# More gathers replaced by single-row copies on the SP and ScalarE queues, row addresses shifted ahead on VectorE, a 127-row load cut in two, and a small operand moved to PSUM

## The chip, the core and the metric

The kernel runs on one core of a Trainium2 chip. A core has five engines with an instruction queue each: TensorE (PE in the profile, with its weight loads as PEld), VectorE (DVE), ScalarE (ACT), GpSimd (POOL) and SyncE (SP)[...]. SP, ACT and POOL can issue DMAs. The metric is device time in microseconds (us) of one execution; lower is better. "Before" is the kernel without the change, "after" the one with it.

## What is computed

A layer norm, a two-layer graph network and a residual, on 12,500 nodes of 128 features and 200,000 edges sorted by destination. From the reference, cut:

```python
h = jnp.maximum(_layernorm(x), 0.0)                       # the network's node_features
wsum = segment_sum(edge_weight_raw, dst); deg = segment_sum(ones, dst)
w = edge_weight_raw / jnp.maximum(wsum, EPS)[dst]
feat = relu(node_features @ W_pool + b_pool)
msg = feat[src] * w[:, None]
neigh = where(deg > 0, segment_max(msg, dst), 0.0)
rst = node_features @ W1_self + neigh @ W1_neigh + b1
h = relu(rst / jnp.maximum(norm(rst), EPS))
neigh2 = segment_sum(h[src] * w[:, None], dst) / jnp.maximum(deg, 1.0)
out = x + relu(h @ W2_self + neigh2 @ W2_neigh + b2)
```

All is in float32. Twice, a row of 512 bytes is fetched for each of the 200,000 edges: `feat[src]` in layer 1, `h[src]` in layer 2.

## The kernel before

The program has three stages, each with an order of instructions written out by hand (`manual_schedule`). An engine executes its own instructions in that order; engines wait for each other by semaphores that the framework sets from the tiles' use.

**Preparation.** Nodes are taken in 25 groups of up to 4 x 128. Turn `i` of the loop at line 380 starts group `i` and finishes group `i - 3`. DVE takes mean and variance (L417, L418), writes the negative mean to `offs` (L422), and a turn later multiplies it by the reciprocal deviation (L400, L402); ACT takes the deviation (L420) and applies both (`xn`, L406); PE transposes and multiplies by W_pool; DVE adds the bias (`fb`, L385); POOL takes the maximum with 0 (`fr`, L388, three buffers); SP stores it to the table `feat_d` in HBM (L389). Beside this, DVE prepares edge lists (`edges1`, from L216 on). The lists lie 512 edges to a partition. `load_edges` (L119) loads them; the first 128 rows of `dst` are one row (L116) and a piece of 127, because each row carries its neighbours' values. They stand on ACT's queue between the loads of `src` and of the weights, while SP loads x (L132).

**Layer 1.** Edges are taken in 391 groups of 512, a group as 4 chunks of 128. In turn `i`, POOL issues the indirect gathers of group `i` (L503), each of which fetches 128 rows of `feat_d` by the indices in `srcT`; the tiles `gt` have 8 buffers. ACT multiplies by the edge weight (`gs`, L629), PE transposes, and DVE runs a scan with maximum (L636) that takes a mask from `kt`, which SP loads for each group, 4 turns ahead (L601). In later turns the last element of each segment is moved to its node's column: DVE makes a selection matrix (`sel`, L653), PE multiplies, ACT copies into `agg` (L678). Each fourth turn or so, when 128 nodes are whole, `nodes1` begins the node's part as a chain of six pieces, one a turn; in the fourth of them SP stores `h` to the table `h_d` (L551). Background jobs on the edge lists run on DVE in odd turns.

**Layer 2** has the same gathers from `h_d`, DVE makes `s` from the weights and positions (L711, L713), PE multiplies (`pa`, L731), DVE adds into `agg` (L736), and `nodes2` stores the result (L573). A last part, for inputs out of the expected form, is skipped at run time.

**Rows.** `Rows` (L456) spares POOL some gathers. For certain groups the first chunk is fetched by 128 single-row DMAs into a tile `ga` (two buffers). `load` of the 128 source indices into `ri` is L495; a queue then reads 8 of them into registers (L487), and for each computes the row's place and issues a copy of one row (L491). `every`, the distance of such groups, is 24 in layer 1 (SP alone) and 10 in layer 2 (SP and ACT, half each). The copies of a group are spread over the `every - 2` turns that begin `every` turns ahead. Their call stands at the head of a turn. Eight semaphores serve all DMAs of SP and ACT in rotation: a copy waits until the one eight places before it in the program has landed.

Of the kernel before, what the change touches and what calls it, by code (L numbers as in the profile page):

```python
# [7 lines left out]
F32 = mybir.dt.float32  # L8
BF16 = mybir.dt.bfloat16
I16 = mybir.dt.int16  # L10
I32 = mybir.dt.int32
AF = mybir.ActivationFunctionType
OP = mybir.AluOpType
# [4 lines left out]
P = 128  # L18
D = 128
G = 512  # L20
Q = 4
# [6 lines left out]
SLOW_B = 64  # L28
RB = 8
BL = 8  # L30
# [4 lines left out]
def gnn_kernel(ctx, tc, x, src, dst, ew, w_pool, b_pool, w1s, w1n, b1, w2s, w2n, b2, out):  # L35
# [13 lines left out]
    nc = tc.nc  # L49
    N = x.shape[0]  # L50
    E = src.shape[0]
    HI = -(-N // P)
# [3 lines left out]
    NG = GF + 1  # L56
# [56 lines left out]
    def load_edges(eng, a, tl, lead, t):  # L113
        o, k, row = t * P * G, min(P, GF - t * P), 0
        if lead and t == 0:
            eng.dma_start(tl[0:1, 0, 1:], a[None, 0:G + 1])  # L116
            row, o, k = 1, G, k - 1
        if k > 0:
            eng.dma_start(  # L119
                tl[row:row + k, t, :],  # L120
                bass.AP(tensor=a.tensor, offset=a.offset + o - lead, ap=[[G, k], [1, G + 2 * lead]]))
        if t == NT - 1:
            r = GF % P
            eng.dma_start(tl[r:r + 1, t, :TAIL + lead], a[None, E - TAIL - lead:E])
# [48 lines left out]
    shift = {}  # L173
# [206 lines left out]
    for i in range(len(groups) + 3):  # L380
# [16 lines left out]
        if at[1]:  # L397
            t0, n = at[1]
            rstd = rstds.pop(i - 1)
            nc.vector.reciprocal(rstd, rstd)  # L400
            off = offs.pop(i - 1)
            nc.vector.tensor_tensor(off, off, rstd, OP.mult)  # L402
            xn = wk.tile([P, Q, D], F32, name="xn")
# [6 lines left out]
        if at[0]:  # L410
# [9 lines left out]
            nc.scalar.activation(rstd, mv[:, :, 1], AF.Sqrt, bias=eps)  # L420
            offs[i] = wk.tile([P, Q], F32, name="off")
            nc.vector.tensor_scalar(offs[i], mv[:, :, 0], -1.0, None, op0=OP.mult)  # L422
# [33 lines left out]
    class Rows:  # L456


        def __init__(self, pool, table_d, every, engines):
            self.pool, self.table_d, self.every, self.engines = pool, table_d, every, engines  # L460
            self.tiles, self.todo, self.index = {}, [], {}

        def takes(self, g):
            return g >= 2 * self.every and g % self.every == 0 and g < NG - 16

        def tile(self, g):
            return self.tiles.pop(g)

        def turn(self, i):

            span = self.every
            g = i + span
            if self.takes(g):
                ga = self.tiles[g] = self.pool.tile([P, D], F32, name="ga", bufs=2)
                ri = self.index.pop(g)
                each = P // len(self.engines)
                self.todo = []
                for r in range(0, each, RB):
                    for e, eng in enumerate(self.engines):
                        self.todo.append((eng, ri, ga, e * each + r))  # L480
                self.steps = [len(self.todo) * k // (span - 2) for k in range(span - 1)]
            now = []
            if self.todo:
                n = self.steps[1] - self.steps[0]
                now, self.todo, self.steps = self.todo[:n], self.todo[n:], self.steps[1:]
            for eng, ri, ga, r in now:
                _, at = nc.values_load_multi_w_load_instructions(  # L487
                    ri[0:1, r:r + RB], [eng.engine], min_val=0, max_val=N - 1,
                    skip_runtime_bounds_check_because="sources of edges are nodes, as the gathers have it")
                for k in range(RB):  # L490
                    eng.dma_start(ga[r + k:r + k + 1, :], self.table_d[bass.ds(at[k], 1), :])  # L491
            g = i + span + 1
            if self.takes(g):
                self.index[g] = self.pool.tile([1, P], I32, name="ri", bufs=1)
                nc.sync.dma_start(self.index[g], src[None, g * G:g * G + P])  # L495

# [35 lines left out]

    def nodes1(wk, ps, t, nT, store):

# [14 lines left out]
        nc.vector.tensor_scalar(h, r, 0.0, ss, op0=OP.max, op1=OP.mult)  # L549
        if store:  # L550
            nc.sync.dma_start(h_d[t * P:(t + 1) * P, :], h)  # L551
        yield
        ph = ps.tile([P, P], F32, name="pn")
        nc.tensor.transpose(ph, h, ident)
# [25 lines left out]
    with tc.manual_schedule(), tc.tile_pool(name="ew", bufs=3) as wk, \  # L580
# [31 lines left out]
        carry = NEG  # L612
        byrow = Rows(wk, feat_d, 24, [nc.sync])
        for i in range(max(turn) + 6):
            byrow.turn(i)
            node_stage(5)
            if i + AHEAD < NG:
# [45 lines left out]
            if i in turn:  # L663
                n = turn[i]
                st = nodes1(wk, ps, n, agg[:, n * P:(n + 1) * P], True)
                next(st)
                busy[i + 1, 1] = st
# [12 lines left out]
            if 0 <= g < NG:  # L680
# [3 lines left out]
                for j, k in chunks:  # L684
                    nc.tensor.matmul(pas[g], rows[:k, j, :], sel[:k, j, :], start=j == 0,  # L685
                                     stop=j == len(chunks) - 1)
            node_stage(2)
            if i % 2:
                side_step()
        assert not busy  # L690
        i = NG
# [3 lines left out]
    with tc.manual_schedule(), tc.tile_pool(name="ew2", bufs=3) as wk, \  # L695
# [6 lines left out]
        late = None  # L702
        byrow = Rows(wk, h_d, 10, [nc.sync, nc.scalar])
        for i in range(max(turn) + 2):
            byrow.turn(i)
            if i < NG:
                gts[i] = gather(gp, h_d, i, byrow)
# [150 lines left out]
```

## Time and profile before

| | |
|---|---|
| runs | 4005.57, 4009.53, 4017.18 us; median 4009.53 |
| profiled execution | 4009.92 us, span 4007.7 us (2.2 us around it) |
| first gather of layer 1, first of layer 2, end of the last | 108.7, 2088.7, 3995.6 us |
| busy: PE, PEld, DVE, ACT, POOL | 59%, 44%, 42%, 22%, 74% |
| PE's clock, mean granted | 0.512 |
| HBM traffic | 73 GB/s over the span |
| gathers | 1549 of `feat_d`, 1527 of `h_d` |
| row copies | SP 1792 of `feat_d` and 2304 of `h_d`; ACT 2304 of `h_d` |

A group of the profile is a source line, an engine, an operation, the tiles it writes and reads, and how often it ran; behind the bar stand the busy time, the mean in ns, and the engine's idle time before it with what ended that. "issue" means that the engine waited for nothing the profile shows. SPq and ACTq are the queues' sequencers, which wait, compute registers and issue DMAs; this is not in the engines' busy time. In the view of one line the durations are least, median and greatest in ns, followed by the first and last start in us.

### The profile page before, as it was taken

What the parts mean: (1) busy time and instruction counts of PE and PEld (TensorE: products, weight loads), DVE (VectorE), ACT (ScalarE), POOL (GpSimd) and SP (SyncE); (2) the same over time, 40 slices, a digit from 0 to 9 for tenths busy, and PEclk for the clock granted to TensorE, in tenths of its full rate; (3) what the DMA queues carried; (4) which work ended last, traced back from release to release, by engine and by line L of the source; (5) the groups of instructions that cost most, each with busy time, mean ns of one, the idle gap of its engine ahead of it and who ended that gap; (6) DMA issues with size and microseconds to landing.
All of it is one profiled execution on the core that took longest, in us unless ns stands there. A gap on an engine that the chain in (4) does not pass through costs nothing. (4 is left out here: it accounts for less than half of the span.)

```text
span 4007.7 us, 52674 instructions
## 1 busy us (share of the span) xinstructions
PE 2370.1 (59%) x8349; PEld 1781.3 (44%) x8349; DVE 1670.9 (42%) x4620; ACT 889.9 (22%) x2907; POOL 2982.5 (74%) x3135
## 2 busy tenths in 40 slices
PE   6566666666666666666655555555555555555555
PEld 4344444444444444444444444444444444444444
DVE  8566666666666655555551111122121212112111
ACT  6344443444444444444430000000000000000000
POOL 4777777777777777777767777777777777777776
PEclk8555555555555555555555555555555555555555
DMA  5333333333333333333322222222222222222222
GB/s 150 88 81 84 81 82 82 81 81 83 82 84 82 82 83 84 83 84 83 83 62 59 61 61 62 61 62 62 61 62 61 62 61 61 62 62 61 61 61 55
DMA packets 238964, 295.25 MB, mean 74 GB/s; under 512 B 67603, under 2 KB 188228, under 8 KB 238614
## 3 DMA queue, kind: packets, MB, share of 16 engines
q0 software_dynamic: 98432, 201.72, 19.0%
q1 hardware_dynamic: 134868, 87.97, 8.0%
q10 hardware_dynamic: 5314, 2.11, 0.2%
q14 instruction: 278, 2.28, 0.2%
q8 instruction: 72, 1.18, 0.1%
HBM read 271.75 MB, written 19.77 MB: 73 GB/s over the span
## 5 line engine op out<-in xcount | busy, mean ns | idle before, releaser
L503 POOL DMA_INDIRECT gt<-feat_d,srcT x1549 | 1490.2, 962 | 474.2 <-issue 413.3
L503 POOL DMA_INDIRECT gt<-h_d,srcT x1527 | 1441.7, 944 | 483.1 <-issue 435.9
L731 PE MATMUL pa<-s,gt 128*128 128x48 f32 x3054 | 979.6, 423 | 840.7 <-DMA gt<-h_d,srcT 764.4
L731 PEld LDWEIGHTS pa<-s,gt 128*128 128x128 f32 x3054 | 765.1, 312 | 1057.8 <-DMA gt<-h_d,srcT 844.0
L630 PE MATMUL pm<-ident,gs 128*128 128x128 f32 x1563 | 681.2, 463 | 748.8 <-ACT gs L629 738.4
L629 ACT ACTIVATE gs<-gt,ewT 128x128 f32<-128x128 f32 x1549 | 608.3, 400 | 1007.7 <-DMA gt<-feat_d,srcT 995.2
L636 DVE TENSOR_TENSOR_SCAN pm<-kt,carry,pm 128x512 f32<-128x512 bf16 x390 | 502.0, 1287 | 728.5 <-PE pm L630 726.7
L630 PEld LDWEIGHTS pm<-ident,gs 128*128 128x128 f32 x1563 | 316.4, 208 | 1065.6 <-ACT gs L629 1054.9
L736 DVE TENSOR_TENSOR agg<-pa,agg 128x48 f32 x391 | 81.4, 208 | 1505.9 <-PE pa L731 1031.8
L685 PEld LDWEIGHTS pa<-sel,rows 128*128 128x128 f32 x1564 | 374.5, 329 | 34.5 <-ACT agg L678 34.1
L685 PE MATMUL pa<-sel,rows 128*128 128x48 f32 x1564 | 377.0, 390 | 0.9 <-ACT agg L678 0.9
L673 PE MATMUL pr<-ident,sc 128*128 128x128 f32 x782 | 246.8, 419 | 0.0
L653 DVE TENSOR_SCALAR sel<-cols,lastT,invT 128x48 f32<-128x48 f32 x782 | 206.7, 316 | 0.0
L645 DVE COPY_PREDICATED sc<-kt,pm 128x256 f32<-128x256 int16 x391 | 173.1, 443 | 13.3
L673 PEld LDWEIGHTS pr<-ident,sc 128*128 128x128 f32 x782 | 170.7, 227 | 0.1
L644 DVE COPY sc<-pm 128x256 f32<-128x256 f32 x391 | 162.1, 415 | 0.0
L713 DVE TENSOR_TENSOR s<-hit,w2T 128x192 f32<-128x192 f32 x391 | 139.7, 357 | 13.5
L660 ACT ACTIVATE rows<-pr 128x256 f32<-128x256 f32 x392 | 142.6, 364 | 1.0 <-PE pr L673 1.0
L711 DVE TENSOR_TENSOR hit<-iota,locT 128x192 f32<-128x192 f32 x391 | 139.1, 356 | 0.1
L678 ACT ACTIVATE agg<-pa 128x48 f32 x391 | 79.8, 204 | 140.1 <-PE pn L531 136.7
L530 PE MATMUL pn<-w_2s,hT 128*128 128x128 f32 x196 | 74.4, 484 | 0.0
L640 DVE COPY carry<-pm 128x1 f32<-128x1 f32 x390 | 61.6, 158 | 13.4
(143 smaller groups left out, 1274.2 us busy)
## 6 DMA issues: line engine op xcount, KB each, us to landing
kt<-keep_d SPq DMA_DIRECT2D x390, 128.0 KB
ga<-h_d SPq DMA_DIRECT2D x2304, 0.5 KB
ga<-h_d ACTq DMA_DIRECT2D x2304, 0.5 KB
ga<-feat_d SPq DMA_DIRECT2D x1792, 0.5 KB
gt<-feat_d,srcT POOLq DMA_INDIRECT x1549
gt<-h_d,srcT POOLq DMA_INDIRECT x1527
h_d<-h SPq DMA_DIRECT2D x98, 64.0 KB
xr<-in_x SPq DMA_DIRECT2D x97, 64.0 KB
```

The lines of the kernel that those rows point to most:

```text
L503: nc.gpsimd.indirect_dma_start(out=gt[:k, j, :], out_offset=None, in_=table_d[:, :], in_offset=bass.IndirectOffsetOnAxis(ap=srcT[:k, t, j, ...
L629: nc.scalar.activation(gs[:k, j, :], rows_j, AF.Copy, scale=ewT[:k, t, j, r:r + 1])
L630: nc.tensor.transpose(pms[i][:, j * P:j * P + k], gs[:k, j, :], ident[:k, :k])
L636: nc.vector.tensor_tensor_scan(pm[:, :ne], kt[:, :ne], pm[:, :ne], carry, op0=OP.add, op1=OP.max)
L644: nc.vector.tensor_copy(sc[:, :ne // 2], two[:, :, 1])
L645: nc.vector.copy_predicated(sc[:, :ne // 2], new[:, :, 1], two[:, :, 0])
L653: nc.vector.tensor_scalar(sels[g][:k, j, :], cols[:k, 1, :], lastT[:k, t, j, r:r + 1], invT[:k, t, j, r:r + 1], op0=OP.is_equal, op1=OP.mult)
L660: nc.scalar.activation(rws[g][:k, j, :], pr[:k, j, :], AF.Copy)
L673: nc.tensor.transpose(prs[g][:k, j, :], sc[:, j * P:j * P + k], ident)
L685: nc.tensor.matmul(pas[g], rows[:k, j, :], sel[:k, j, :], start=j == 0, stop=j == len(chunks) - 1)
L713: nc.vector.tensor_tensor(ss[i], hit, w2T[:, t, :, r:r + 1].to_broadcast([P, Q, LW]), OP.mult)
L731: nc.tensor.matmul(pas[g], rows_j, s[:k, j, :], start=j == 0, stop=j == len(chunks) - 1)
```

## The change

1. `Rows` takes each twelfth group in layer 1 from group 12 on (96 rows by SP in batches of 8, 32 by ACT in batches of 4), and each eighth in layer 2 from group 8 on (64 and 64, in batches of 8). Groups are taken up to 386. The batches are spread over all `every` turns that begin `every + 1` turns ahead. In layer 1 ACT's batches stand at the end of a turn; in layer 2 both queues' stand at its head.
2. The row numbers are shifted left by 9 on DVE, two turns before the first is used there, so that a queue reads the byte's place and issues the copy with it, both sides viewed as bytes. Two halves of one tile hold the lists in turn.
3. `load_edges` issues a list as a part of a multiple of 16 rows and a rest: the 127 rows become 112 and 15.
4. In the preparation the negative mean is written to PSUM, and the product with the reciprocal deviation to a new tile in SBUF.
5. The store of `h` comes one piece later, but for the last four node groups.

```diff
-        if k > 0:
-            eng.dma_start(
-                tl[row:row + k, t, :],
-                bass.AP(tensor=a.tensor, offset=a.offset + o - lead, ap=[[G, k], [1, G + 2 * lead]]))
+        for n in (k // 16 * 16, k % 16):
+            if n > 0:
+                eng.dma_start(
+                    tl[row:row + n, t, :],
+                    bass.AP(tensor=a.tensor, offset=a.offset + o - lead, ap=[[G, n], [1, G + 2 * lead]]))
+            o, row = o + n * G, row + n
...
-            off = offs.pop(i - 1)
-            nc.vector.tensor_tensor(off, off, rstd, OP.mult)
+            off = wk.tile([P, Q], F32, name="off")
+            nc.vector.tensor_tensor(off, offs.pop(i - 1), rstd, OP.mult)
...
-            offs[i] = wk.tile([P, Q], F32, name="off")
+            offs[i] = ps.tile([P, Q], F32, name="neg")
...
+        def __init__(self, pool, table_d, every, share):
+            self.pool, self.every, self.share = pool, every, share
+            self.bytes = table_d[:, :].bitcast(U8).rearrange("n b -> (n b)")
+            self.tiles, self.index, self.plan = {}, {}, {}
+            self.ri = pool.tile([64, P], I32, name="ri", bufs=1)
+            for g in range(every, NG - 4, every):
+                first = g - every - 1
+                at = 0
+                for eng, n, rb in share:
+                    for s in range(n // rb):
+                        turn = max(first + s * every // (n // rb), 0)
+                        self.plan.setdefault(turn, []).append((g, eng, at, rb))
+                        at += rb
+            self.turn(-2)
+            self.turn(-1)
...
         def takes(self, g):
-            return g >= 2 * self.every and g % self.every == 0 and g < NG - 16
+            return g % self.every == 0 and self.every <= g < NG - 4
+
+        def turn(self, i):
+            for g, lead, step in ((i + self.every + 2, -1, self.shift), (i + self.every + 3, -2, self.load)):
+                if i == lead:
+                    step(self.every)
+                elif i >= 0 and g > self.every and self.takes(g):
+                    step(g)
+
+        def load(self, g):
+            r = g // self.every % 2 * 32
+            self.index[g] = self.ri[r:r + 1, :]
+            nc.sync.dma_start(self.index[g], src[None, g * G:g * G + P])
+
+        def shift(self, g):
+            nc.vector.tensor_scalar(self.index[g], self.index[g], ROW_SHIFT, None, op0=OP.logical_shift_left)
+
+        def rows(self, i, engine):
+            for g, eng, r, rb in self.plan.get(i, ()):
+                if eng is not engine:
+                    continue
+                if g not in self.tiles:
+                    self.tiles[g] = self.pool.tile([P, D], F32, name="ga", bufs=2)
+                ga, ri = self.tiles[g].bitcast(U8), self.index[g]
+                _, at = nc.values_load_multi_w_load_instructions(
+                    ri[0:1, r:r + rb], [eng.engine], min_val=0, max_val=(N - 1) << ROW_SHIFT, ...)
+                for k in range(rb):
+                    eng.dma_start(ga[r + k:r + k + 1, :], self.bytes[None, bass.ds(at[k], 4 * D)])
...
-        if store:
+        if store and t >= HI - 4:
             nc.sync.dma_start(h_d[t * P:(t + 1) * P, :], h)
         yield
+        if store and t < HI - 4:
+            nc.sync.dma_start(h_d[t * P:(t + 1) * P, :], h)
...
-        byrow = Rows(wk, feat_d, 24, [nc.sync])
+        byrow = Rows(wk, feat_d, 12, [(nc.sync, 96, 8), (nc.scalar, 32, 4)])
         for i in range(max(turn) + 6):
             byrow.turn(i)
+            byrow.rows(i, nc.sync)
...
             node_stage(2)
+            byrow.rows(i, nc.scalar)
             if i % 2:
                 side_step()
...
-        byrow = Rows(wk, h_d, 10, [nc.sync, nc.scalar])
+        byrow = Rows(wk, h_d, 8, [(nc.sync, 64, 8), (nc.scalar, 64, 8)])
         for i in range(max(turn) + 2):
             byrow.turn(i)
+            byrow.rows(i, nc.sync)
+            byrow.rows(i, nc.scalar)
```

More of the change, by code (lines that the diff above doesn't have):

```diff
@@ L11 @@
 I32 = mybir.dt.int32
+U8 = mybir.dt.uint8
 AF = mybir.ActivationFunctionType
@@ L28 @@
 SLOW_B = 64
-RB = 8
+ROW_SHIFT = 9
 BL = 8
@@ L456, in gnn_kernel @@
     class Rows:
-        def __init__(self, pool, table_d, every, engines):
-            self.pool, self.table_d, self.every, self.engines = pool, table_d, every, engines
-            self.tiles, self.todo, self.index = {}, [], {}
-        def takes(self, g):
-            return g >= 2 * self.every and g % self.every == 0 and g < NG - 16
+        def __init__(self, pool, table_d, every, share):
[3 more added lines that the diff above has]
+            self.ri = pool.tile([64, P], I32, name="ri", bufs=1)
+            assert sum(n for _, n, _ in share) == P
+            for g in range(every, NG - 4, every):
[8 more added lines that the diff above has]
+            self.turn(-1)
@@ new lines, in shift @@
+        def shift(self, g):
[8 more added lines that the diff above has]
+                _, at = nc.values_load_multi_w_load_instructions(
+                    ri[0:1, r:r + rb], [eng.engine], min_val=0, max_val=(N - 1) << ROW_SHIFT,
+                    skip_runtime_bounds_check_because="sources of edges are nodes, as the gathers have it")
+                for k in range(rb):
+                    eng.dma_start(ga[r + k:r + k + 1, :], self.bytes[None, bass.ds(at[k], 4 * D)])
@@ L466, in tile @@
         def tile(self, g):
             return self.tiles.pop(g)
[L469 to L495, printed above, removed]
@@ L531, in linear, with nodes1 @@
         return nc.tensor.matmul(po, nT, W[neigh_w], start=False, stop=True)
-    def nodes1(wk, ps, t, nT, store):
+    def nodes1(wk, ps, t, nT, store=True):
         po = ps.tile([P, D], F32, name="pn")
@@ L664, in gnn_kernel @@
                 n = turn[i]
-                st = nodes1(wk, ps, n, agg[:, n * P:(n + 1) * P], True)
+                st = nodes1(wk, ps, n, agg[:, n * P:(n + 1) * P])
                 next(st)
```

## Prediction

> **What bounds the kernel now.** I read the page's groups first, for the engine that is busiest and for what its idle time waits on.
>
> ```profile
> L503 POOL DMA_INDIRECT gt<-feat_d,srcT x1549 | 1490.2, 962 | 474.2 <-issue 413.3
> L503 POOL DMA_INDIRECT gt<-h_d,srcT x1527 | 1441.7, 944 | 483.1 <-issue 435.9
> ```
>
> GpSimd (POOL) issues 3076 indirect gathers of 128 rows. Busy and idle time of the two groups add up to 1964 and 1925 us, nearly the whole span, and the idle part is "issue": it waits for nothing. The timeline of layer 2 shows the beat.
>
> ```profile
> 3035.51 0.94 POOL L503 DMA_INDIRECT gt<-h_d,srcT  x1 [0.30 <-issue]
> 3036.76 0.95 POOL L503 DMA_INDIRECT gt<-h_d,srcT  x1 [0.30 <-issue]
> 3038.01 0.94 POOL L503 DMA_INDIRECT gt<-h_d,srcT  x1 [0.31 <-issue]
> ```
>
> A gather each 1.249 us, 0.94 busy and 0.30 between. From start to start over all gathers the trace gives a mean of 1.249 in layer 2 (longest 1.27) and 1.267 in layer 1, where 62 intervals are over 1.3 us and hold 27 us of excess. So both layers cost the number of gathers times this beat. The table by windows says how far the others are from it.
>
> ```profile
> 110.00:2070.00 1960.00, 1214.74 (x4454) 866.02 (x4455) 1190.71 (x2884) 816.98 (x2719) 1488.28 (x1548) 0.50 0.32 83
> 2088.00:3995.00 1907.00, 1068.61 (x3505) 852.06 (x3506) 385.12 (x1365) 0.00 (x0) 1441.07 (x1527) 0.50 0.22 61
> ```
>
> The columns are window, its length, then PE, PEld, DVE, ACT and POOL busy, the clock, and the DMA share, at most a third. Nobody but POOL is near its limit. What this table leaves out are the sequencers of SP and ACT, which issue single rows. Their own instructions show when one asks for line 491, line 487 and the waits.
>
> ```profile
> L491 SPq FUSED_REGOPS  x4096: 37/37/51, 238.1 to 3870.7; - x196
> L491 SPq MOVE ga<-feat_d x1792: 29/29/38, 238.2 to 1908.1; - x200
> L491 SPq DMA_DIRECT2D ga<-feat_d x1792: 224/228/308, 238.3 to 1908.1; - x200
> L487 SPq TENSOR_LOAD <-ri x512: 524/731/965, 237.3 to 3867.0; - x171
> 1012.09 3.14 SPq L491 DMA_DIRECT2D ga<-feat_d  x8
> SPq L551 <- DVE sel L653: 636.4, 94, 18.9
> ACT gs L629 <- DMA gt<-feat_d,srcT: 994.7, 1171, 2.6
> ```
>
> A row costs SP three instructions; eight rows took 3.14 us from the first issue to the end of the last, so (3.14 - 0.23)/7 = 0.416 us a row. SP waits 636 us in layer 1 for the node results it stores, ACT 995 us for gathers: this is the room that the change will use.
>
> Outside both layers stands the preparation, 108.7 us until the first gather. Its timeline shows two stalls and one repeated delay.
>
> ```profile
> 2.75 0.23 ACTq L119 DMA_DIRECT2D dr<-in_dst  x1
> 4.69 6.15 ACTq L119 DMA_DIRECT2D er<-in_edge_weight  x1
> 10.87 1.28 ACT L420 ACT_TABLE_LOAD   x1 [10.87 <-issue]
> 22.00 0.15 DVE L216 CAST r_first<-dr 128x1 f32<-128x1 int32 x1 [4.99 <-DMA dr<-in_dst]
> ...
> 36.03 0.16 DVE L402 TENSOR_TENSOR off<-off,rstd 128x4 f32<-128x4 f32 x1
> 78.22 1.49 POOL L388 TENSOR_SCALAR fr<-fb 128x512 f32<-128x512 f32 x1 [0.22 <-DVE rstd L400]
> 78.25 0.59 DVE L402 TENSOR_TENSOR off<-off,rstd 128x4 f32<-128x4 f32 x1
> ...
> L402 DVE TENSOR_TENSOR off<-off,rstd x25: 161/592/604, 12.7 to 101.1; 128x4 f32<-128x4 f32 x25
> ```
>
> The destination list (127 rows of 2 KB) is issued at 2.75 and lands at 22.0, and its semaphore gets one update where the 128-row loads get 16, in the trace. While it drains, the next issue holds ACT for 6.15 us, SP's loads of x are held too (the last is issued at 32.3), and the DMA share falls to 0.09 between 16 and 20 us. And L402, 0.16 us when alone, takes 0.59 in 21 of its 25 runs, each 0.03 us after POOL's L388 began.
>
> **The change part by part.** Fewer gathers. Before, the first chunk of groups 48, 72 .. 360 in layer 1 and 20, 30 .. 370 in layer 2 comes by rows: 14 and 36. After, it is 12, 24 .. 384 and 8, 16 .. 384: 32 and 48. So 18 and 12 gathers go. At 1.249 us, layer 1 gives 22.5 us and layer 2 15.0. The 27 us of excess stay: they lie mostly under DVE's background jobs on the edge lists, which are unchanged.
>
> What stands in for them. Rows rise from 1792 to 4096 in layer 1 (3072 on SP, 1024 on ACT) and from 4608 to 6144 in layer 2. I cost this at nothing, and these are the covers. The pre-shifted places remove the register multiply: 0.037 us and its gap of some 0.04, leaving 0.33 a row. SP in layer 1 then does in every turn one load of places (0.72 + 0.05), 8 rows (2.66), a kt issue (0.41) and a quarter of a store (0.10): 3.95 us, against 47 gathers per 12 turns, 4.89 us. In layer 2 it is 0.83 + 2.66 and a quarter of two issues (0.21), 3.7 of 31 x 1.249/8 = 4.84 us. ACT in layer 1 gets, per 12 turns, 32 rows and 8 loads of 0.83 (ACT's median of L487) + 0.05: 17.6 us in 58.7, where it waits 2.55 us a group, 30.6, for gathers. The rows go behind the turn's last evacuation, so what queues behind them is the next turn's scaling, whose gathers come 1.25 us apart: at 2.2 us a batch it has caught up by the fourth. ACT in layer 2 has no other work: 3.5 of 4.84 us. If these covers go, POOL still has 8 gather buffers, about 35 us, before it feels it.
>
> The price of a byte-typed row of 512 elements is in no row of the trace. From below: 0.26, if the MOVE went too. From above: the 128-row issues of line 119 took 0.446 where the row takes 0.228, so 0.33 + 0.22 = 0.55. I take 0.33, since the copy stays one run of 512 bytes on one partition, and keep both ends.
>
> New waits. A copy waits for the copy eight places earlier in program order, on whatever queue, so in layer 1 ACT's and SP's rows now wait for each other. A row landed about 1.4 us after its issue in the trace (layer 2). ACT's first row of a turn needs SP's second of that turn, SP's fifth the ACT's first of the turn before: two landings, 2.8 us plus issues, inside 4.89. Layer 2 has had the same alternation of eight and eight: there 24 SP rows took 12.04 us when catching up, 4.0 a batch, also inside. SP's rows end at turn g-2 now instead of g-3 in layer 2; PE may wait there more often than today's three times, with 44% idle and 8 buffers behind it: nothing. The node store one turn later frees SP of part of its 636 us; the last four stores stay, so the 18.9 us from the last gather of layer 1 to the first of layer 2 stay too. Index loads (50 before, 80 after, 0.23 us on SP) are in the noise of the above.
>
> The shifts. 80 tensor_scalars of 1x128 on DVE, some 0.15 us each. Here a rule speaks against the change. The trace has 774 tensor_scalars of L653, SBUF to SBUF, under layer 1's gathers; two fall in a long interval. The Trainium skill, "SBUF — State Buffer", Who interferes with whom, says tensor_scalar can enter a mode that takes the port pair shared with GpSimd and blocks the other for its whole instruction. By the rule up to 80 x 0.15 = 12 us come back; by the row 0.1. I take the row, and keep 12 in the range.
>
> The preparation. (a) The list in 112 and 15 rows. The 128-row loads of the same queue land at 4.7 to 9.4 us beside the same traffic, so I put it at 10. What 15 rows do is not in the trace: on one engine 19 x 15/127 = 2.3 us, while the skill's "DMA: Bandwidth & Descriptors", Queues, rings and completion order, lets a copy run on the largest count up to 16 that divides its rows, 15 here. Either is in time. ACT's last issue then ends near 5.8 (its semaphore at 4.7, an issue, and one more), the table load near 7.0, so the first rstd comes at 7.0 instead of 12.17: 5.1 us. From there to L216 the work takes as long as from 12.17 to 17.02, so L216 runs at about 12 rather than 22.00: 10 us. SP takes part of it back: `fr` has three buffers, so the fourth L388 waits for the first store, and SP stores only after its x loads. These need some 7.3 MB at 0.28 MB/us, the rate of the windows at 24 to 32 us, so the store would land near 30 instead of 37, where the quick pipeline would have wanted it at 24. DVE runs on until it needs fb again, at about 29.8, and then waits some 1.7 us. (b) L402 with one operand in PSUM: in the trace L385, one operand in PSUM, shows no such delay beside L388 or L409, so I take 0.16, saving 0.43. Four of these 21 lie in the first part (1.6 us). For the other 17, the chain rstd, hT and xn on ACT is 2.7 us against DVE's 3.11 - 0.43 = 2.68, just not binding; at PE's half clock it sometimes is, so 0.35 each, 6.0 us. Sum: 10 + 1.6 - 1.7 + 6.0, say 16 us. From below 5 us, if L402 stays slow and the store holds everything from 30 us on; from above 20.
>
> Sum: 16 + 22.5 + 15.0 = 53.5. The profiled execution is 4009.92, its span 4007.7 and 2.2 around; 4009.9 - 53.5 = 3956.4. The median of the runs, 4009.53, is 0.4 below it: 3956.
>
> **The rivals.** Little from the preparation (5 us): 4009.9 - 5 - 37.5 = 3967. For it: SP's x loads stand before its stores. Against: the idle DMA engines at 16 to 20 us show that the loads are held by the one list.
>
> SP becomes the bound: the slower side. Both layers then cost 390 x (8r + 1.29) + 391 x (8r + 1.04) = 6248 r + 910 us, with r the price of a row. Today's two layers less what the preparation gives, 1961 + 1906 + 16 = 3883, is reached at r = 0.476: from there it is slower. At r = 0.55 it is 4346, and the kernel 4473. For it: 8 rows in every turn of layer 1, where before 16 of 24 turns had them, and a copy of a kind that has no row. Against: 0.416 holds today with the multiply in it.
>
> ACT and SP hold each other in layer 1 beyond the buffers. At 5.2 us a turn it is 390 x 5.2 - 1961 = +67, and 4009.9 - 16 - 15 + 67 = 4046. It decides from 5.05 us a turn. Against it: 2.8 us of landings in 4.89.
>
> That the change does not do what it says is excluded for the gathers: the built program has 1531 and 1515.
>
> **How the numbers follow.** The sum as told 0.84 (3945 to 3969 with the bounds of the shifts and the preparation), little preparation 0.07, SP the bound 0.05, the hold 0.04. 0.3% is 12 us, about what a measurement of this kernel can tell from no change. Faster has the first two, 0.91; slower the last two less a mild end of each, 0.08; within 0.01. The range reaches from 3942, all preparation and less excess, to 3976, the little preparation with some hold.
>
> **What would show it.** Right: POOL's two groups x1531 and x1515 with 1.25 us from start to start; first gather near 92 us; L216's row without its wait; L402 near 0.16 throughout; no FUSED_REGOPS, rows 0.33 us apart; ACT's waits for gathers smaller by some 500 us. Wrong: POOL's idle time put down to ACT's scaling, PE or a DMA instead of issue; intervals over 1.3 us in layer 2; rows more than 0.45 us apart.

## The result, and the profile after

The changed kernel takes 3950.8 us (median of four runs, 3949.8 to 3955.7) where the kernel before takes 4008.2 (four runs): 0.9855 of the time, 95% interval 0.9837 to 0.9873. The prediction was 3956, within 3942 to 3976. The profiled execution took 3949.8 us, with a span of 3947.9, 59.8 shorter than before.

In ten of the twelve experiments below every kernel was slow, the kernel before at 5500 to 5600 us (one chip gave 5517 for it and later 4008, so the cause, which was not found, lies outside the kernels); a ratio is therefore always to the kernel before on the same chip at the same time.

First the groups of the page of the changed kernel: busy time and mean, then idle time before them and what ended it.

```profile
L525 POOL DMA_INDIRECT gt<-feat_d,srcT x1531 | 1466.1, 958 | 469.5 <-issue 391.4
L525 POOL DMA_INDIRECT gt<-h_d,srcT x1515 | 1429.5, 944 | 483.1 <-issue 388.3
...
L500 DVE TENSOR_SCALAR ri<-ri 1x128 int32<-1x128 int32 x80 | 18.2, 227 | 505.1 <-DMA ri<-in_src 495.7
```

GpSimd still waits for "issue" and little else (its other waits within the layers are of 0.3 us at most), with 18 and 12 gathers fewer. From the start of one gather to the start of the next, the median is 1.249 us in both layers, as before. New is the third line: DVE stands 505 us in all before its 80 shifts. The windows of the two layers (length, then PE, PEld, DVE, ACT and POOL busy):

```profile
92.00:2024.00 1932.00, 1020.60 (x4447) 850.47 (x4447) 1179.13 (x2902) 722.47 (x2717) 1465.23 (x1531) 0.54 0.32 84
2045.00:3936.00 1891.00, 1061.99 (x3504) 850.23 (x3504) 395.18 (x1413) 0.00 (x0) 1428.41 (x1514) 0.50 0.22 62
```

The layers take 1932 and 1891 us where they took 1960 and 1907. In layer 1 PE is busy for 1021 us instead of 1215 and ACT for 722 instead of 817 with nearly the same number of instructions. I read this as work done in bursts, where instructions overlap and count less as busy time; that was not tested. What makes the bursts shows in SP's row instructions (lowest, median and highest time in ns), in the timeline and in the waits (total, times, longest):

```profile
L514 SPq MOVE ga<-feat_d x3072: 29/29/38, 98.2 to 2010.8; - x192
L514 SPq DMA_DIRECT2D ga<-feat_d x3072: 227/228/474, 98.3 to 2010.9; - x192
```

```profile
1000.17 2.54 SPq L514 DMA_DIRECT2D ga<-feat_d  x8
1000.98 0.29 DVE L500 TENSOR_SCALAR ri<-ri 1x128 int32<-1x128 int32 x1 [14.06 <-DMA ri<-in_src]
...
2012.80 0.40 ACT L654 ACTIVATE gs<-ga,ewT 128x128 f32<-128x128 f32 x1 [16.12 <-DMA ga<-feat_d]
```

```profile
SPq L514 <- DMA ga<-h_d: 301.4, 398, 5.4
SPq L514 <- DMA ga<-feat_d: 257.8, 285, 5.4
PE pm L655 <- DVE sc L670: 497.3, 43, 17.2
```

The multiply is gone, and the eight rows at 1000.17 take (2.54 - 0.23) / 7 = 0.33 us each. But this is one of the fast batches. SP waits 559 us in all for the landing of another row copy, and over its 384 batches of layer 1 a row takes 0.38 us in the median and 0.43 in the mean, as much as the 0.43 of the kernel before with its multiply: what the shift saved there, the waits took back. In layer 2 its median and mean are 0.38, where the kernel before had 0.43 and 0.44.

SP runs more than two turns behind DVE (the index that DVE stood ready for at 986.92 was issued at 999.00), so DVE stands for an index 14 us long at a time, and PE waits 497 us for DVE in 43 pieces, the longest as long as DVE's own. ScalarE's wait for gathers fell from 995 to 134 us, but it now waits 302 us for row copies: before the first scaling of each of the 32 row groups it stands until the last rows have landed, 3 to 6 us for most, 15 for the first and 16 for the last, which is the line at 2012.80. In the kernel before, the last row was issued 12 to 14 us ahead, and ScalarE never stood for it.

From a gather's issue to its scaling in layer 1 it is now 10.3 us in the median and up to 23, where it was 2.6 and 5.2. This lag swings with each row group and hardly grows: the longest is 20.6 us in the first twelfth of the gathers and 22.9 in the last. Eight gather buffers are some 39 us of gathers, so GpSimd does not feel it. The chain of work that ended last, followed back, shows the same: in layer 2 it is GpSimd's gathers (45% of that time, and DMA of gathers 30%), but in layer 1 SP's row copies (13%), PE, DVE and the loads of `kt`, with GpSimd at 2%. In layer 1 the rows keep pace with the gathers, with little to spare.

The preparation, in the timeline (start, length, engine; in brackets the idle time before):

```profile
2.81 2.59 ACTq L121 DMA_DIRECT2D dr<-in_dst  x2
5.43 1.09 ACTq L121 DMA_DIRECT2D er<-in_edge_weight  x1
6.55 1.28 ACT L423 ACT_TABLE_LOAD   x1 [6.55 <-DMA dr<-in_dst]
12.79 0.15 DVE L219 CAST r_first<-dr 128x1 f32<-128x1 int32 x1
91.93 1.16 POOL L525 DMA_INDIRECT gt<-feat_d,srcT  x1 [2.75 <-issue]
```

```profile
L405 DVE TENSOR_TENSOR off<-neg,rstd x25: 160/161/164, 8.4 to 83.9; 128x4 f32<-128x4 f32 x25
```

The list no longer holds ScalarE (1.09 us for 6.15) or DVE's cast (12.79 without a wait for 22.00 after 4.99). L405, the multiplication by the reciprocal deviation, is short in all its 25 runs. The first gather comes at 91.93 instead of 108.72. And between the layers, before and after:

```profile
2069.88 0.91 POOL L503 DMA_INDIRECT gt<-feat_d,srcT  x1 [0.30 <-issue]
2088.74 0.95 POOL L503 DMA_INDIRECT gt<-h_d,srcT  x1 [17.96 <-issue]
```

```profile
2023.88 0.91 POOL L525 DMA_INDIRECT gt<-feat_d,srcT  x1 [0.30 <-issue]
2045.80 0.96 POOL L525 DMA_INDIRECT gt<-h_d,srcT  x1 [21.01 <-DMA ri<-in_src]
```

From start to start 18.9 us have become 21.9. The wait at 2012.80 is where they come from, as far as the traces show: it is for the rows of group 384, the seventh from the end, and ScalarE then scales four groups in one go and is still 4 to 6 us behind at the last four gathers, where it was 2 to 4. The span's change in parts: preparation -16.8, layer 1 -29.2, between the layers +3.1, layer 2 -15.3, after the last gather -1.6 (13.07 to 11.47); together -59.8.

### The profile page after: what moved, and what is told of

It is laid out like the page before. It is cut to its first block, busy times and chain, and to the rows that moved or that the text cites. A ratio compares the mean times of both kernels' runs of the same rounds, so it can differ in the third digit from the quotient of the medians.

```text
span 3947.9 us, 55088 instructions
## 1 busy us (share of the span) xinstructions
PE 2163.9 (55%) x8349; PEld 1764.2 (45%) x8349; DVE 1664.7 (42%) x4700; ACT 795.0 (20%) x2907; POOL 2946.2 (75%) x3105
## 3 DMA queue, kind: packets, MB, share of 16 engines
q0 software_dynamic: 97472, 199.75, 18.8%
## 4 chain that ended last, share of the span: by engine, by line
DMA 24%; POOL 23%; issue 17%; SPq 10%; PE 9%; DVE 7%; ACT 5%; ACTq 4%; POOLq 0%; DVEq 0%
POOL gt L525 23%; DMA gt<-h_d,srcT 14%; SPq L514 6%; PE pm L655 4%; DMA kt<-keep_d 4%; DVE pm L661 4%; DMA ga<-feat_d 3%; ACTq L514 3%; ACT gs L654 3%; SPq L510 2%; DMA ri<-in_src 1%; DMA gt<-feat_d,srcT 1%; PE pa L710 1%; SPq L625 1%; PE pn L552 1%
## 5 line engine op out<-in xcount | busy, mean ns | idle before, releaser
L525 POOL DMA_INDIRECT gt<-feat_d,srcT x1531 | 1466.1, 958 | 469.5 <-issue 391.4
L759 PE MATMUL pa<-s,gt 128*128 128x48 f32 x3030 | 967.9, 423 | 826.6 <-DMA gt<-h_d,srcT 736.1
L655 PE MATMUL pm<-ident,gs 128*128 128x128 f32 x1563 | 484.0, 439 | 902.0 <-DVE sc L670 497.3
L655 PEld LDWEIGHTS pm<-ident,gs 128*128 128x128 f32 x1563 | 288.5, 199 | 1038.2 <-issue 483.4
L654 ACT ACTIVATE gs<-gt,ewT 128x128 f32<-128x128 f32 x1531 | 503.6, 392 | 357.0 <-DMA ga<-feat_d 200.6
L710 PEld LDWEIGHTS pa<-sel,rows 128*128 128x128 f32 x1564 | 352.5, 311 | 35.9 <-ACT agg L703 34.0
L710 PE MATMUL pa<-sel,rows 128*128 128x48 f32 x1564 | 358.0, 375 | 2.6 <-ACT agg L703 1.1
L500 DVE TENSOR_SCALAR ri<-ri 1x128 int32<-1x128 int32 x80 | 18.2, 227 | 505.1 <-DMA ri<-in_src 495.7
L565 ACT ACTIVATE sq<-r 128x128 f32<-128x128 f32 x98 | 29.7, 303 | 375.7 <-DVE r L561 375.7
```

The source lines that it names most:

```text
L525: nc.gpsimd.indirect_dma_start(out=gt[:k, j, :], out_offset=None, in_=table_d[:, :], in_offset=bass.IndirectOffsetOnAxis(ap=srcT[:k, t, j, ...
L654: nc.scalar.activation(gs[:k, j, :], rows_j, AF.Copy, scale=ewT[:k, t, j, r:r + 1])
L655: nc.tensor.transpose(pms[i][:, j * P:j * P + k], gs[:k, j, :], ident[:k, :k])
L759: nc.tensor.matmul(pas[g], rows_j, s[:k, j, :], start=j == 0, stop=j == len(chunks) - 1)
```

## The experiments

My theory: GpSimd's beat (the 1.249 us from one gather to the next) times the number of gathers makes the layers, the preparation is a separate sum of two parts, and the rows are free as long as SP and ScalarE can issue them within a turn. The rivals: the parts of the preparation overlap or give back; the waits that are hidden in layer 1 cost something after all; SP is at its edge.

**split_only.** The kernel before with the first part of the preparation alone:

```diff
-        if k > 0:
+        for n in (k // 16 * 16, k % 16):
```

> The kernel before with the row lists in even parts alone. By the prediction's step: the list's issue falls from 6.15 to about 1 us on ScalarE, L216 goes from 22.0 to about 12, SP's feature stores take 1.7 us back: the first gather 8.3 us earlier, at 100.4, and 4008.2 - 8 = 4000. Rival, SP's loads of x hold everything behind L216: the store wait takes most of it back, first gather 105 to 108, time 4005 to 4008.

5515.7 us, 0.9991 of before (0.9978 to 1.0004): nothing that can be told by the time, in layers that take 5300 us there. The timeline of the preparation tells more:

```profile
2.76 2.71 ACTq L120 DMA_DIRECT2D dr<-in_dst  x2
5.50 0.60 ACTq L120 DMA_DIRECT2D er<-in_edge_weight  x1
13.14 0.15 DVE L218 CAST r_first<-dr 128x1 f32<-128x1 int32 x1
100.67 1.16 POOL L505 DMA_INDIRECT gt<-feat_d,srcT  x1 [2.75 <-issue]
```

```profile
L404 DVE TENSOR_TENSOR off<-off,rstd x25: 161/592/607, 8.0 to 92.6; 128x4 f32<-128x4 f32 x25
```

The first gather is 8.05 us earlier than the 108.72 of the kernel before. L404, the same multiplication, stays slow, as it should.

**neg_only.** The kernel before with the second part alone. Of the core's two on-chip memories, `wk` tiles lie in SBUF and `ps` tiles in PSUM:

```diff
-            off = offs.pop(i - 1)
-            nc.vector.tensor_tensor(off, off, rstd, OP.mult)
+            off = wk.tile([P, Q], F32, name="off")
+            nc.vector.tensor_tensor(off, offs.pop(i - 1), rstd, OP.mult)
...
-            offs[i] = wk.tile([P, Q], F32, name="off")
+            offs[i] = ps.tile([P, Q], F32, name="neg")
```

> The kernel before with the negative mean in PSUM alone. By the prediction's step: 0.43 us off each L402, 0.35 of it on the path 17 times and 0.43 four times: 7.6 us, first gather at 101. Rival one, the preparation is set by x's loads and the late list until about 37 us, so only what comes after counts: 6 us, first gather 102.7. Rival two, the pace there is ScalarE's chain and not DVE: below 3 us, first gather 106 or later.

5517.8 us, 0.9987 (0.9969 to 1.0004). From its trace:

```profile
L402 DVE TENSOR_TENSOR off<-neg,rstd x25: 160/161/163, 13.4 to 92.2; 128x4 f32<-128x4 f32 x25
```

```profile
4.71 6.78 ACTq L119 DMA_DIRECT2D er<-in_edge_weight  x1
...
99.81 1.16 POOL L503 DMA_INDIRECT gt<-feat_d,srcT  x1 [2.31 <-DMA feat_d<-fr]
```

The list still holds ScalarE, here for 6.78 us, and the first gather is 8.9 us earlier: 21 times 0.43 is 9.0, so nearly all of the delay lay on the path. The edit also gives the product a tile of its own; whether that or PSUM removes the delay was not tested apart. The two parts make 8.05 + 8.9 = 16.95 us, and both together 16.8: they add up.

**rows_only.** The changed kernel with both of these undone (cut).

```diff
-        for n in (k // 16 * 16, k % 16):
+        if k > 0:
...
-            offs[i] = ps.tile([P, Q], F32, name="neg")
+            offs[i] = wk.tile([P, Q], F32, name="off")
```

> The changed kernel with the row lists in one part and the negative mean in SBUF, as before; both layers as changed. If GpSimd's beat sets the layers and the preparation is a separate sum, the first gather is back at 108 to 109 us and the layers as in the changed kernel: 3950.8 + 16.8 = 3967.6 us. If the layers gain only by the 30 gathers that are no longer issued (the sum of the prediction), 4008.2 - 37.5 = 3970.7. If the later start lets SP and ScalarE catch up in layer 1, or takes cover from it, layer 1 differs from 1932 us between first and last gather by more than 3 us.

5873.8 us, 1.065 of before (1.063 to 1.068), so my expectation of 3967.6 could not be judged. The first gather is at 110.6, 1.9 us after that of the kernel before with the same preparation. Taken from this base, the parts above are 10.0 and 10.8 us, 20.8 in sum, and 18.7 together. So the two parts account for the whole, and they add up within about 2 us; nothing finer can be said from single profiles.

**f32_rows, after_again, no_rows, few_rows.** What the rows cost where SP's instructions are dear. after_again is the changed kernel itself. The diffs are cut: f32_rows also leaves out the shift on DVE, and no_rows also plans no rows and loads no indices.

```diff
# f32_rows
-                ga, ri = self.tiles[g].bitcast(U8), self.index[g]
+                ga, ri = self.tiles[g], self.index[g]
-                    eng.dma_start(ga[r + k:r + k + 1, :], self.bytes[None, bass.ds(at[k], 4 * D)])
+                    eng.dma_start(ga[r + k:r + k + 1, :], self.table_d[bass.ds(at[k], 1), :])
# no_rows
-            return g % self.every == 0 and self.every <= g < NG - 4
+            return False
# few_rows
-        byrow = Rows(wk, feat_d, 12, [(nc.sync, 96, 8), (nc.scalar, 32, 4)])
+        byrow = Rows(wk, feat_d, 48, [(nc.sync, 96, 8), (nc.scalar, 32, 4)])
-        byrow = Rows(wk, h_d, 8, [(nc.sync, 64, 8), (nc.scalar, 64, 8)])
+        byrow = Rows(wk, h_d, 32, [(nc.sync, 64, 8), (nc.scalar, 64, 8)])
```

> The changed kernel with rows addressed as before the change: the copies are f32 rows, the row number is multiplied at each issue by SP or ScalarE, and the shifts on DVE are left out; same groups, same shares. At the kernel before's price of a row, 0.416 us, SP needs 8 x 0.416 + 1.29 = 4.62 us of a turn of 4.89 in layer 1 and as much in layer 2: GpSimd still sets the beat, and the time is 3951 within 5 (the places made ahead then bring nothing to the time at this share). Rival: the waits for a DMA lane, which already stretch the rows, leave too little: SP becomes the bound in layer 1, 0.2 us a turn or more, from 4030 up.

> The changed kernel with every chunk gathered by GpSimd: no group is read by rows, so SP and ScalarE issue no row copies, no index loads, and DVE no shifts. If GpSimd's beat is the bound and each gather left out is worth 1.249 us, 80 more gathers than in the changed kernel make 3950.8 + 80 x 1.249 = 4050.7 us, within 8. The same is expected on a chip where the other kernels need 5500 to 5900 us, if the stalls of 0.7 us at SP's and ScalarE's instructions there do their harm through the row copies: then it is the fastest of all there. Rival: the stalls reach the beat without the rows, through the keep rows on SP's queue and ScalarE's own register instructions; then it stays above 4300 there.

> The changed kernel with a quarter of its row groups: each 48th of layer 1, each 32nd of layer 2 (8 and 12 groups instead of 32 and 48). By the beat, 60 more gathers than the changed kernel: 3950.8 + 60 x 1.249 = 4025.7. On a chip with the stalls, 2 to 4 rows in a turn instead of 8 to 16 leave SP and ScalarE time, and the same number should come; if SP is still the bound it lies above 4200.

> The changed kernel itself, on the chip of these runs. Where the kernel before needs 4008 us, 3951. Where the kernel before needs 5500 to 5600, SP is the bound and the rows cost more than the gathers they replace: about 5860, 5 to 6% slower than before, as rows_only and early_index.

| kernel | rows | us | of before (95%) |
|---|---|---|---|
| no_rows | 0 | 4709 | 0.853 (0.852 to 0.855) |
| few_rows | 2560 | 4780 | 0.867 (0.865 to 0.868) |
| before | 6400, three instructions each | 5517 | 1 |
| after_again | 10240, two each | 5855 | 1.062 (1.058 to 1.067) |
| f32_rows | 10240, three each | 6376 | 1.155 (1.153 to 1.157) |

The changed kernel itself is slower than before here, on the side of the rival "SP becomes the bound". GpSimd now waits for ScalarE to free a gather buffer (first line; the tile `rows` there is a result of PE that ScalarE copies, not the row copies). The durations of SP's MOVE, lowest, median and highest, show stalls (second line, for 29/29/38 above); 975 of SP's 6146 MOVEs took over 0.6 us:

```profile
POOL gt L525 <- ACT rows L685: 1020.4, 97, 25.6
```

```profile
L514 SPq MOVE ga<-feat_d x3072: 1/29/1440, 98.2 to 3101.4; - x192
```

Taking the multiply from the issue, with all that f32_rows undoes, is worth 521 us between the last two rows (the kernels before beside them differ by 6), some 0.05 us for each of 10240 copies. My expectation for no_rows failed: 4051 was expected and its rival, above 4300, came. Without any rows, and with hardly an instruction of SP over 0.6 us (22 of 1298), its layers still take 2350 and 2210 us, and all engines but GpSimd stand together for up to 24 us. So SP's stalls are not the whole cause, which stays open. few_rows went the same way, to the side above 4200. The order of the five is what can be used: the more rows, and the more instructions to a row, the slower.

**early_index and dense_10_6.** The index of layer 1 six turns earlier; more groups.

```diff
# early_index
-            for g, lead, step in (..., (i + self.every + 3, -2, self.load)):
+            for g, lead, step in (..., (i + self.every + self.ahead, -2, self.load)):   # ahead = 9 in layer 1
# dense_10_6
-        byrow = Rows(wk, feat_d, 12, [(nc.sync, 96, 8), (nc.scalar, 32, 4)])
+        byrow = Rows(wk, feat_d, 10, [(nc.sync, 96, 8), (nc.scalar, 32, 4)])
-        byrow = Rows(wk, h_d, 8, [(nc.sync, 64, 8), (nc.scalar, 64, 8)])
+        byrow = Rows(wk, h_d, 6, [(nc.sync, 64, 8), (nc.scalar, 64, 8)])
```

> The changed kernel with the row indices of layer 1 fetched six turns earlier on SP's queue, shifts and rows where they were. In the changed kernel DVE stands some 14 us before each shift of layer 1 (456 us in 31 waits) until the index has landed; here it has landed long before. If GpSimd's beat alone sets layer 1, those waits were covered: 3951 within 5 us, and DVE's wait at the shift falls below 30 us with no gain. If the waits cost something, as the lag of ScalarE behind the gathers and the 3 us more between the layers would let them, the gap between the layers goes back to about 19 us and layer 1 loses its gaps: 3 to 15 us faster. On a chip whose SP needs 0.7 us at many instructions, as in the runs of rows_only, SP is the bound, the fetch's place doesn't count, and the time is near 5860.

> The changed kernel with more row groups: each tenth of layer 1 (38 instead of 32), each sixth of layer 2 (64 instead of 48), same shares of SP and ScalarE. Where GpSimd's beat is the bound, 22 gathers fewer: 3950.8 - 22 x 1.249 = 3923, if SP's 9.6 rows a turn of layer 1 (9.6 x 0.33 + 1.31 = 4.48 us of 4.88) and 10.7 of layer 2 (4.6) still fit. Rival: the lanes and the index wait have used the cover up already; layer 1 goes over the beat and the time is 3960 to 4050. On a chip where before needs 5500, SP is the bound and 22 groups of rows more make it slower than the 5855 of the changed kernel, near 6100.

5872 and 6370 us, 1.050 (1.048 to 1.052) and 1.152 (1.149 to 1.155), near the 5860 expected for the first and worse than the 6100 for the second. The early fetch does what it should: DVE's wait for the index in layer 1, 752 us in after_again, is gone. But layer 1 is no shorter (3002 us for 2987), so that wait was not what held it there. 22 more groups cost. What both would do where GpSimd sets the beat these two do not tell.

**stores_five.** The wait that the split list left in the preparation.

```diff
-            fr = wk.tile([P, Q, D], F32, name="fr", bufs=3)
+            fr = wk.tile([P, Q, D], F32, name="fr", bufs=5)
# and layer 1's last row group, 384, is gathered: g < NG - 16 for g < NG - 4
```

> The changed kernel with five fr buffers instead of three in the preparation, so that the fourth and fifth L391 need not wait for the first feature store; and in layer 1 the last row group, 384, is gathered (31 groups by rows). In the changed kernel GpSimd waited 7.0 us for that store and DVE 1.4 us behind it. By the prediction's term the wait is worth 1.4 to 1.7 us: first gather at 90.3 to 90.6 instead of 91.9. Rival one: the wait also delays DVE's later work, which then fills its idle time; first gather at 88 or earlier. Rival two: the pace after 28 us is set by x's loads and the chain behind them, and the first gather stays at 91.5 to 92.3. Between the layers, if the last row group makes the 3 us, the gap goes back from 21.9 to about 19 us, where GpSimd sets the beat; where SP is the bound the gap stays above 40. The whole: 3950.8 - 1.5 - 3 + 1.2, about 3947, or where before needs 5500, 5855 within 20.

5848 us, 1.059 (1.054 to 1.063). Below, the wait of GpSimd in the changed kernel, then the windows from 28 to 36 us of the changed kernel and of this one, and this one's first gather:

```profile
POOL fr L391 <- DMA feat_d<-fr: 7.0, 1, 7.0
```

```profile
28.00:36.00 8.00, 6.50 (x27) 5.06 (x25) 6.21 (x27) 5.03 (x13) 5.05 (x5) 0.50 0.73 211
```

```profile
28.00:36.00 8.00, 6.63 (x27) 5.83 (x28) 7.45 (x35) 5.93 (x15) 5.31 (x5) 0.50 0.95 288
```

```profile
90.58 1.16 POOL L525 DMA_INDIRECT gt<-feat_d,srcT  x1 [2.75 <-issue]
```

DVE does 1.24 us more in this stretch, and the first gather is at 90.58: 1.35 us before the changed kernel, of which 0.57 are there already at the first L391, ahead of any wait for a buffer. The eight profiles with three buffers lie at 91.1 to 92.3, 91.8 in the mean, and the two with five, this and dense_early, at 90.6 and 91.0. So lifting GpSimd's 7.0 us of waiting is worth about 1 us, near DVE's part of it (put at 1.4) and far from the whole. The gap between the layers (37.0, for 56.4 in after_again and 35.1 in no_rows) tells nothing at this scatter.

**fixed_rows.** The copies alone, without register work: the row numbers are written into the program (so they are not the edges' sources), and the built program has no loads and no MOVEs for them. `row` stands for the formula in the code.

```diff
-                    eng.dma_start(ga[r + k:r + k + 1, :], self.bytes[None, bass.ds(at[k], 4 * D)])
+                    row = (g * 509 + (r + k) * 97) % N
+                    eng.dma_start(ga[r + k:r + k + 1, :], self.table_d[row:row + 1, :])
```

> The changed kernel with the same number of row copies on the same queues, in the same turns, but from row numbers that are written into the program: the rows read are not the edges' sources, and SP and ScalarE neither load the numbers nor move one per copy, nor wait for DVE's shift. One instruction per row is left of two (three in f32_rows). Where before needs 4008, GpSimd's beat is the bound: 3951 within 8. Where before needs 5500: if the short register instructions are what SP cannot issue in time there, the step from three to two, which was worth 6376 - 5855 = 521 us, comes again, with the loads on top: 5330 or lower. Rival: the copies themselves, by their issue or the wait for a lane, are the price; then it stays above 5700.

The kernel before took 4008.4 us beside it, and this one 3947.2 (3944.9 to 3947.6), 0.9846 of it (0.9830 to 0.9863), for 0.9855 of the changed kernel; 3951 within 8 was expected. SP has 6100 of its 14600 instructions fewer, and the kernel moves by less than 4 us: they are off the path at this share. Its waits on SP, and the first gather of layer 2:

```profile
SPq L514 <- DMA ga<-h_d: 649.3, 874, 9.3
SPq L514 <- DMA ga<-feat_d: 537.2, 303, 6.9
SPq L514 <- DMA kt<-keep_d: 181.3, 237, 1.9
```

```profile
2040.97 0.95 POOL L525 DMA_INDIRECT gt<-h_d,srcT  x1 [17.80 <-DMA ri<-in_src]
```

Most of the issue time that SP saves turns into waits for landings: 1186 us for row copies and 181 for the loads of `kt` here, 559 and 30 in the changed kernel. And the gap between the layers is 18.7 us again. The lag of ScalarE behind the gathers is 4.5 us in the median, for 10.3; its wait for the rows of group 384 is 10.5 us, for 16.1, and by the last four gathers it is no later than in the kernel before (2.4 to 3.6 us).

**dense_early.** 21 more groups by rows than the changed kernel, indices fetched five turns earlier in layer 1, rows there only up to group 370, and five `fr` buffers (cut); the kernel that should have been faster than both.

```diff
-        byrow = Rows(wk, feat_d, 12, [(nc.sync, 96, 8), (nc.scalar, 32, 4)])
+        byrow = Rows(wk, feat_d, 10, [(nc.sync, 96, 8), (nc.scalar, 32, 4)], ahead=8, stop=NG - 16)
-        byrow = Rows(wk, h_d, 8, [(nc.sync, 64, 8), (nc.scalar, 64, 8)])
+        byrow = Rows(wk, h_d, 6, [(nc.sync, 64, 8), (nc.scalar, 64, 8)])
```

> The changed kernel with more row groups (each tenth of layer 1 up to 370, 37 for 32; each sixth of layer 2, 64 for 48), layer 1's indices fetched five turns earlier, and five fr buffers. Where before needs 4008 us and GpSimd's beat holds: 21 gathers fewer, 26.2; the preparation 1.4; the gap between the layers back to about 19, 3.1; together 3950.8 - 30.7 = 3920. SP needs 9.6 x 0.33 + 1.31 = 4.48 us of a turn of 4.88 in layer 1 and 10.7 x 0.33 + 1.06 = 4.6 in layer 2, by issue alone. Rival: the eight lanes are what SP waits for (1368 us in fixed_rows, whose issue was shorter), and 9.6 and 10.7 rows a turn beside ScalarE's go over the beat: layer 1 or layer 2 then shows gather intervals well over 1.249 and the time is 3960 to 4050. Where before needs 5500: SP is the bound, 6350 as dense_10_6.

4433 us, 1.107 of before (1.104 to 1.109), with the kernel before at 4009 beside it. The rival came true, and by more than its own numbers, 3960 to 4050. The shares of its chain and its gathers, its waits and its windows:

```profile
DMA 20%; ACTq 17%; issue 5%; SPq 5%; PE 1%; DVE 1%; POOL 0%; DVEq 0%; ACT 0%
...
L525 POOL DMA_INDIRECT gt<-feat_d,srcT x1526 | 1457.6, 955 | 683.2 <-issue 373.8
L525 POOL DMA_INDIRECT gt<-h_d,srcT x1499 | 1414.4, 944 | 741.5 <-issue 404.9
```

```profile
POOL gt L525 <- PE pa L759: 302.3, 119, 6.0
POOL gt L525 <- ACT rows L685: 230.1, 49, 9.0
```

```profile
92.00:2228.00 2136.00, 1050.36 (x4453) 861.28 (x4454) 1187.92 (x2921) 717.51 (x2719) 1455.73 (x1525) 0.53 0.29 76
2247.00:4384.00 2137.00, 764.26 (x3448) 745.22 (x3448) 385.77 (x1411) 0.00 (x0) 1413.46 (x1498) 0.50 0.19 55
```

GpSimd has fewer gathers and more idle time (741 us for 483 in layer 2), and the chain, where it could be followed, goes through row copies and ScalarE's queue instead of POOL. The early fetch is not to blame: in layer 1 DVE no longer waits for an index (456 us in the changed kernel), and layer 2, where density alone differs, grew as well, from 1891 to 2137 us.

A turn is 2136 / 390 = 5.48 us in layer 1 with 9.6 rows on SP, and 2137 / 391 = 5.47 in layer 2 with 10.7 on each queue. In layer 1 SP's own instructions and the gaps of at most 0.15 us between them fill 83% of that, 4.5 us, near the 4.48 of my sum; 0.9 us are waits. In layer 2 they fill 88% on SP and 90% on ScalarE, 4.8 and 4.9 us: there the issue alone reaches the beat's 1499 x 1.249 / 391 = 4.79, and waits come on top. Put into the formulas of the expectation, 9.6 r + 1.31 = 5.48 and 10.7 r + 1.06 = 5.47, a row costs an estimated r = 0.43 and 0.41 us with its waits, not 0.33. By this estimate eight rows make 4.8 us of 4.89 in layer 1: the changed kernel stands close to the edge. The lag tells the same: its longest in a twelfth of layer 1 is 39 us in the first and 44 to 46 in all later ones, so the buffers are used up at once and stay so. The gap between the layers is 18.8 us here, with no rows in the last twenty groups.

## Why the prediction was right

The mechanism held: GpSimd kept its beat of 1.249 us, issued 30 gathers fewer, and began earlier. Of the terms, the waits and the end of layer 1 were sized wrongly. 53.5 us were predicted and 59.8 measured between the two profiles (57.4 between the medians); that an unforeseen loss of 3.1 us and unforeseen gains of some 8 partly cancel is luck.

The beat and the count, layer 2: 15.0 predicted, 15.3 measured, for 12 gathers. Layer 1: 22.5 predicted for 18 gathers, 29.2 measured; 22.5 of it is the count, and 6.2 is excess that I took as fixed: intervals over 1.3 us fell from 62 to 52 and their excess from 27.2 to 21.0 us (19.9 in fixed_rows). DVE's work is spread otherwise in the changed kernel, by its waits; whether that lessens the excess was not separated.

The preparation: 16 predicted, 16.8 measured. By its terms, the list was put at 10 less 1.7 for the store wait, 8.3, and gave 8.05; the wait left in it, put at 1.7, was worth about 1 when it was lifted. What 15 rows do, which the prediction left open, the trace of the changed kernel shows: after a first mark at its issue, their copy left 15 landing marks, from 9.8 to 12.6 us, where the 127 rows had left one, at 21.9. This agrees with the Trainium skill's "DMA: Bandwidth & Descriptors", where the largest count up to 16 that divides the rows stands in the section Why a DMA increments its semaphore by 16 and not by 1, not in the one that the prediction names. The negative mean was put at 7.6 and gave 8.9; 0.35 us for each of 17 runs was too careful, since 21 times the full 0.43 make 9.0. Both readings are single profiles, with the 2 us of doubt that rows_only leaves.

The shifts: 0.1 us by the row, up to 12 by the rule. None of the 80 shifts lies in a gather interval over 1.3 us, so going by the row was right here. What the shifts did cost is another thing, which the prediction did not see: not their 0.23 us but their place. The index is loaded on SP's queue behind rows that wait, and DVE stands for it, 31 times in layer 1 and some 15 us each time.

The cover on SP and ScalarE: 3.95 of 4.89 us in layer 1 and 3.7 of 4.84 in layer 2 were predicted; in the trace SP's instructions and gaps of at most 0.15 us fill 80% and 77%, 3.9 and 3.7 us. So the issue was sized well. The step that was mis-sized is the waits, "two landings, 2.8 us plus issues, inside 4.89": with them a row costs 0.43 us in the mean of layer 1 and not 0.33, SP falls more than two turns behind, DVE waits for its indices and ScalarE for its rows. 121 of SP's 384 batches there have rows more than 0.45 us apart, which the prediction had named as a sign of being wrong. When those engines stand, SP does a turn in 4.2 us (from 991.66 to 995.90 and to 1000.17) and catches up. That the time still came out is due to the eight gather buffers, named as the last cover: the changed kernel uses up to 23 of their 39 us, and dense_early shows that a quarter more groups by rows (101 for 80) uses them up. The rival of SP and ScalarE holding each other was thus close. Its threshold is not what its own sum gives, though: (1961 + 16 + 15) / 390 is 5.11 us a turn and not 5.05.

Between the layers: unchanged was predicted, 3.1 us more were measured. "The last four stores stay" was true, but relative to the last gather everything that is left to finish comes some 3 us later (the last copy into `agg` at 14.8 us after it instead of 11.7, the last store at 19.4 instead of 16.3). The two kernels with no lag left at the end of the layer, fixed_rows and dense_early, have 18.7 and 18.8. Here hidden lag cost nothing until all engines had to finish the layer, and there it was paid.

After the last gather: no change predicted, 1.6 us less measured (11.5 in fixed_rows too), which no experiment took apart.

## What to carry to other kernels

When single copies take work from a bound engine, price them with their waits for landings and not only by the pace within a batch: 0.33 us became 0.43 in the mean as the queue filled, and where each group had gained 1.25 us, a quarter more groups cost 482. A lag that buffers hide is free in the middle of a stage and can be paid at its end, so the last groups of a stage are the wrong ones to slow. Two small repairs of a preparation are best judged by the time of one event behind it, the first gather here: they moved it by 8 to 11 us each where whole runs could tell nothing.

## What the runs showed of the hardware that was not expected

One copy of 127 rows held the issue of the next on its queue for 6.15 us in the kernel before and 6.78 in neg_only; as 112 and 15 rows it held it for 1.09 in the changed kernel and 0.60 in split_only. One operand moved from SBUF to PSUM, with the result in a tile of its own, took a DVE operation of 128x4 from 592 to 161 ns beside GpSimd's 1.49 us operation (neg_only), so the delay was 0.43 us and not the other's whole length.
